# A 16-stage network on one core: the steps of its first attention in a written order, with the projections copied out of PSUM

## Chip, cores, metric

One NeuronCore of a Trainium2 chip. The metric is the device time of one execution in microseconds (us). All tensors of this stage are float32.

## The reference, cut to what matters

The network takes a tensor of 8 sequences ("batches", b) x 512 tokens x 128 features through sixteen layers, attention and feed-forward in turn, each behind a layer norm and with a residual. The change touches the first layer, a causal linear attention with 16 heads of 8 features:

```python
x = L0_attn_a_X                                    # (8, 512, 128)
x = x + _L0_attn_a_ref(_layernorm(x), Wq, Wv, q_norm_w, v_norm_w)
x = x + _L0_ffn_ref(_layernorm(x), ...)            # mixture of experts, top 2 of 8

def _L0_attn_a_ref(X, Wq, Wv, q_norm_w, v_norm_w):
    K = X.reshape(B, L, H, d)
    Q = rms_norm_multihead((X @ Wq.T).reshape(B, L, H, d), q_norm_w)
    V = rms_norm_multihead((X @ Wv.T).reshape(B, L, H, d), v_norm_w)
    W = jnp.cumsum(jnp.einsum('blhd,blhe->blhde', K, V), axis=1)
    return jnp.einsum('blhd,blhde->blhe', Q, W).reshape(B, L, D)
```

The keys are the normalised input itself. Queries and values are projected and RMS-normalised per head. Nothing of the mathematics changes.

## The kernel before

**Tiling.** A batch of 512 tokens is four tiles of 128 tokens; a tile t is 128 partitions x 128 features. For each batch the stage does two groups of steps and a tail.

*Begin steps* (`begin_steps`, L306 on): layer norm of the batch (`self.norm`, L202: statistics on VectorE L198 and L199, the root on GpSimd L180 and L184, the scaling on VectorE L207); transposes of the four tiles into one PSUM bank (L255) and a copy out by ScalarE (L257); `project(0)` and `project(1)`, each two tiles times the query and value weights (L316), squared by ScalarE (L326) and summed per head by VectorE (L327); `scales` (VectorE L337, the root on ScalarE L339, VectorE L341 to L344); `normalise(0)` and `normalise(1)`, which multiply the projections, read from PSUM, by the scales into `q` (L352) and into a block-diagonal value tile `vm` (L359, two buffers, one for even and one for odd batches); `queries` (transposes L369, four ScalarE copies with a head mask into `qm`, L375, and one into `qT`, L376).

*Chunk steps* (`chunk_steps`, L389 on), per tile t: `scores(t)` (TensorE L397 into two double-bank PSUM tiles `sc`, of which the pool holds two; half of them is masked and copied out by VectorE L406, the other half is copied by ScalarE L409 and masked by GpSimd L410); `carry(t)` (TensorE L423, VectorE L431, for t > 0 GpSimd L433), the running state; `weigh(t)` (for t > 0 TensorE L442, then 32-column matmuls L453) into one PSUM bank `o` that stays open for all four tiles; `copy` (ScalarE L464).

*Tail*: `finish` (transposes L470 and VectorE L174, the residual), then the steps in `ended`, which are the layer norm and the router scores of the mixture of experts that follows: statistics (L198, L180, L184), the shift (VectorE L239), the scaling (ScalarE L244), a store of the normalised batch to DRAM (issued by ScalarE's queue, L553), the transposes (L255, L257), and the router's matmuls (L561) with their sum on VectorE (L571).

**What sets the order.** The stage is under a manual schedule: every engine runs its instructions in the order in which the Python code issues them and waits at the head of its queue until the inputs and the buffer of the next one are there. The Python order is made by `together` (L498): the chunk steps of batch b are spread evenly, the tail of batch b-1 over the first 80% of them, the begin steps of batch b+1 over all of them. The main round of batch b thus holds the chunk steps of b, the tail of b-1 and all begin steps of b+1; these must be done before the next round begins with `scores(0)` of b+1. A step with several engines issues to all of them at once. The pool of single PSUM banks holds four; each half of a projection holds one from `project` until `normalise` has read it, and `o` holds one through the round.

After the last batch's tail the mixture of experts begins with VectorE work on the router scores of all batches (L620 on).

Of the kernel before, what the change touches and what calls it, by code (L numbers as in the profile page):

```python
# [22 lines left out]
F32 = mybir.dt.float32  # L23
# [6 lines left out]
P = 128  # L30
B, S, D, H, HD = 8, 512, 128, 16, 8
NT = S // P
# [4 lines left out]
LN_EPS = 1e-5  # L37
# [45 lines left out]
class Net:  # L83
# [102 lines left out]
    def stats(self, src, eps):  # L186

        nc = self.nc
        mv = self.moments(src)
        rs = self.small([P, NT], "rstd")  # L190
        self.rsqrt(rs, mv[:, :, 1], eps)
        return mv, rs
# [83 lines left out]
        return o.rearrange("p (t d) -> p t d", t=NT)  # L276


    def linear_attention(self):

        nc = self.nc
        w = self.weights("l0a_w")
        with self.tc.tile_pool(name="l0a", bufs=2) as pool, self.tc.tile_pool(
            name="l0a_fix", bufs=1
# [20 lines left out]
            def begin_steps(b, box):  # L307
                xT = self.xTb(b)
                vm = vms[b % 2]

                def project(half):
                    ps = self.av()
                    box["ps", half] = ps
                    for k in range(2):
                        t = 2 * half + k
                        nc.tensor.matmul(  # L316
                            ps[:, k * 256 : (k + 1) * 256],
                            lhsT=xT[:, t * P : (t + 1) * P],
                            rhs=w[:, 0:256],
                            start=True,  # L320
                            stop=True,
                        )
                    if half == 0:
                        box["ss"] = pool.tile([P, P], F32, tag="ss", name="ss")
                    sq = pool.tile([P, 512], F32, tag="sq", name="sq")
                    nc.scalar.activation(sq, ps, AF.Square)  # L326
                    nc.vector.tensor_reduce(  # L327
                        box["ss"][:, half * 64 : (half + 1) * 64],
                        sq.rearrange("p (n d) -> p n d", d=HD),
                        AX.X,  # L330
                        ALU.add,
                    )

                def scales():

                    ss = box["ss"]
                    nc.vector.tensor_scalar(ss, ss, 1.0 / HD, 1e-8, ALU.mult, ALU.add)  # L337
                    r = pool.tile([P, P], F32, tag="r", name="r")
                    nc.scalar.activation(r, ss, AF.Sqrt)  # L339
                    r0 = pool.tile([P, P], F32, tag="r0", name="r0")  # L340
                    nc.vector.reciprocal(r0, r)  # L341
                    nc.vector.tensor_tensor(r, r0, r0, ALU.mult)
                    nc.vector.scalar_tensor_tensor(r, r, -0.5, ss, ALU.mult, ALU.mult)
                    nc.vector.scalar_tensor_tensor(r, r, 1.5, r0, ALU.add, ALU.mult)  # L344
                    box["r"] = r.rearrange("p (t n) -> p t n", t=NT)

                def normalise(half):
                    ps = box["ps", half].rearrange("p (t n d) -> p t n d", t=2, d=HD)
                    r = box["r"][:, 2 * half : 2 * half + 2, :]
                    if half == 0:  # L350
                        box["q"] = pool.tile([P, NT, P], F32, tag="q", name="q")
                    nc.vector.tensor_tensor(  # L352
                        box["q"][:, 2 * half : 2 * half + 2, :].rearrange("p t (n d) -> p t n d", d=HD),
                        ps[:, :, 0:H, :],
                        bc(r[:, :, 0:H], 3, HD),
                        ALU.mult,
                    )
                    for k in range(2):
                        nc.vector.tensor_tensor(  # L359
                            diagonal(vm, 2 * half + k),  # L360
                            ps[:, k, H:32, :].rearrange("p (j r) d -> p r j d", j=4),
                            bc(r[:, k, H:32].rearrange("p (j r) -> p r j", j=4), 3, HD),
                            ALU.mult,
                        )

                def queries():
                    pt = self.m()
                    for t in range(NT):
                        nc.tensor.transpose(pt[:, t * P : (t + 1) * P], box["q"][:, t, :], self.ident)  # L369
                    qm = pool.tile([P, NT, 4, P], F32, tag="qm", name="qm")  # L370
                    box["qm"] = qm
                    box["qT"] = pool.tile([P, S], F32, tag="qT", name="qT")
                    v = pt.rearrange("p (t q) -> p t q", t=NT)
                    for r in range(4):
                        nc.scalar.activation(qm[:, :, r, :], v, AF.Copy, scale=pick[:, r : r + 1])  # L375
                    nc.scalar.activation(box["qT"], pt, AF.Copy, scale=cols[:, 0:1])  # L376

                return [
                    lambda: self.norm(self.xnb(b), self.xb(b)),
                    lambda: self.transposed(xT, self.xnb(b), act=True),  # L380
                    lambda: project(0),
                    lambda: project(1),
                    scales,
                    lambda: normalise(0),
                    lambda: normalise(1),
                    queries,
                ]

            def chunk_steps(b, box):  # L389
                xT, xn, vm = self.xTb(b), self.xnb(b), vms[b % 2]  # L390

                def scores(t):
                    tok = slice(t * P, (t + 1) * P)
                    ss = [self.sc() for _ in range(2)]
                    for j in range(4):
                        rows = slice(32 * j, 32 * j + 32)
                        nc.tensor.matmul(  # L397
                            ss[j // 2][:, j % 2, :],
                            lhsT=xT[rows, tok],
                            rhs=box["qm"][rows, t].rearrange("p r q -> p (r q)"),  # L400
                            start=True,
                            stop=True,
                        )
                    es = [pool.tile([P, 8, P], F32, tag=f"e{k}", name=f"e{k}") for k in range(2)]
                    box["e", t] = es
                    nc.vector.tensor_tensor(  # L406
                        es[0], ss[0].rearrange("p j (r q) -> p (j r) q", r=4), bc(self.cc(C_LIN, P), 1, 8), ALU.mult
                    )
                    nc.scalar.copy(es[1], ss[1].rearrange("p j (r q) -> p (j r) q", r=4))  # L409
                    nc.gpsimd.affine_select(  # L410
                        out=es[1],
                        in_=es[1],
                        pattern=[[0, 8], [1, P]],
                        compare_op=ALU.is_ge,
                        fill=0.0,
                        base=0,
                        channel_multiplier=-1,
                    )
# [51 lines left out]
                        nc.tensor.transpose(pt[:, tok], box["oT"][:, tok], self.ident)  # L470
                    self.add_x(b, pt.rearrange("p (t d) -> p t d", t=NT))

                steps = [lambda: scores(0), lambda: carry(0)]
                for t in range(1, NT):
                    steps += [lambda t=t: scores(t), lambda t=t: weigh(t - 1)]
                    if t < NT - 1:
                        steps.append(lambda t=t: carry(t))
                return steps + [lambda: weigh(NT - 1), copy], finish

            box = {}  # L480
            for f in begin_steps(0, box):
                f()
            tail = None
            for b in range(B):
                main, finish = chunk_steps(b, box)
                sides = []
                if b:
                    sides.append((0.8, [tail] + self.ended(b - 1)))
                if b + 1 < B:
                    box = {}  # L490
                    sides.append((1.0, begin_steps(b + 1, box)))
                self.together(main, *sides)
                tail = finish
            for f in [tail] + self.ended(B - 1):
                f()

    @staticmethod
    def together(main, *sides):  # L498


        at = [((i + 1) / len(main), 0, f) for i, f in enumerate(main)]
        for k, (to, side, *rest) in enumerate(sides):
            begin = rest[0] if rest else 0
            at += [((i + 0.5) / len(side) * (to - begin) + begin, k + 1, f) for i, f in enumerate(side)]
        for _, _, f in sorted(at, key=lambda x: x[:2]):
            f()

# [2100 lines left out]
```

## Time and profile before

| | us |
|---|---|
| median of 3 runs (3680.75 to 3695.16) | 3685.98 |
| the profiled execution | 3678.17 |
| its span, first to last instruction | 3676.3 |
| first projection matmul (L316) starts | 24.29 |
| last router matmul (L561) of the stage ends | 251.97 |
| from one `qm` copy (L375) to the next, batches 3 to 7 | 27.4 |

Times inside the run are counted from the start of the span. The stage is the stretch from 24 to 252 us, 6% of the span. A table by windows gives for each stretch the busy time of each engine (number of instructions in brackets) and the share of full speed that TensorE's clock was granted ("PEclk"). The chain of waits is followed back from the last instruction: at each step to what released it, or to the instruction before it on its engine. Its lines are start, length and what ran; "x8" is eight instructions in a row. TensorE runs each float32 matmul as two instructions, so the four matmuls of `scores(t)` are "x8".

### The profile page before, as it was taken

What the parts mean: (1) busy time and instruction counts of PE and PEld (TensorE: products, weight loads), DVE (VectorE), ACT (ScalarE), POOL (GpSimd) and SP (SyncE); (2) the same over time, 40 slices, a digit from 0 to 9 for tenths busy, and PEclk for the clock granted to TensorE, in tenths of its full rate; (3) what the DMA queues carried; (4) which work ended last, traced back from release to release, by engine and by line L of the source; (5) the groups of instructions that cost most, each with busy time, mean ns of one, the idle gap of its engine ahead of it and who ended that gap; (6) DMA issues with size and microseconds to landing.
All of it is one profiled execution on the core that took longest, in us unless ns stands there. A gap on an engine that the chain in (4) does not pass through costs nothing.

```text
span 3676.3 us, 64102 instructions
## 1 busy us (share of the span) xinstructions
PE 2920.8 (79%) x21332; PEld 1897.3 (52%) x21332; DVE 2503.5 (68%) x7103; ACT 2061.9 (56%) x4054; POOL 1857.4 (51%) x2494
## 2 busy tenths in 40 slices
PE   5757928999958747585655799999999999998886
PEld 3436912333327736483555455666556566555554
DVE  4555328888744357633443689999888899877984
ACT  3422325777732333153333477788887777776773
POOL 3313443332114466244134477667777877665775
PEclk8877958999978967787878899999999999997997
DMA  2001232222001301020013212111121111200000
GB/s 90 13 14 39 66 95 69 65 63 67 28 14 52 102 28 29 15 55 26 27 39 97 83 70 72 67 69 64 62 73 63 57 68 59 74 15 1 7 7 12
DMA packets 129802, 185.03 MB, mean 50 GB/s; under 512 B 19010, under 2 KB 98498, under 8 KB 129478
## 3 DMA queue, kind: packets, MB, share of 16 engines
q1 hardware_dynamic: 98886, 134.27, 10.8%
q0 software_dynamic: 15616, 35.47, 3.7%
q10 hardware_dynamic: 14976, 11.19, 1.1%
q8 instruction: 176, 2.88, 0.3%
q14 instruction: 148, 1.21, 0.1%
HBM read 128.40 MB, written 52.46 MB: 49 GB/s over the span
## 4 chain that ended last, share of the span: by engine, by line
PE 37%; DVE 19%; POOL 15%; DMA 13%; ACT 8%; issue 4%; SPq 2%; another core or an unknown queue 0%; DVEq 0%; ACTq 0%; POOLq 0%
DMA k<-d 9%; PE sc L744 5%; PE av L760 5%; PE av L1065 4%; PE mx L953 3%; PE sc L1034 3%; POOL e L1047 2%; DVE nm L972 2%; ACT e L1044 2%; PE m L255 2%; DMA d<-thirds 2%; SPq L926 2%; POOL left L911 1%; PE up L1321 1%; POOL got L811 1%
## 5 line engine op out<-in xcount | busy, mean ns | idle before, releaser
L1044 ACT ACTIVATE e<-sc 128x1024 f32<-128x1024 f32 (+1 forms) x832 | 745.1, 930 | 158.5 <-PE sc L1034 119.4
L965 DVE TENSOR_REDUCE pm<-mx 128x4 f32<-128x512 f32 (+1 forms) x1152 | 626.2, 592 | 86.5 <-PE mx L953 84.5
L953 PE MATMUL mx<-k,q 126*128 126x512 bf16 (+3 forms) x2048 | 551.3, 327 | 117.0 <-DMA k<-d 104.4
L1034 PE MATMUL sc<-q,k 128*128 128x512 bf16 (+3 forms) x2048 | 446.3, 322 | 20.4 <-ACT e L1044 18.8
L1047 POOL TENSOR_SCALAR_AFFINE_SELECT e<-e 128x256 f32<-128x256 f32 x768 | 295.2, 406 | 198.5 <-ACT e L1044 195.7
L723 POOL DMA_INDIRECT xg<-xd,srci x220 | 210.3, 956 | 365.6 <-DVE srci L716 192.1
L972 DVE TENSOR_REDUCE nm<-mx 128x1 f32<-128x512 f32 x512 | 324.3, 683 | 83.9 <-PE mx L953 81.4
L1065 PE MATMUL av<-e,vaug 128*32 128x512 f32 (+3 forms) x4096 | 366.9, 479 | 1.9 <-ACT e L1044 1.8
L953 PEld LDWEIGHTS <-q 126*128 126x128 bf16 x2048 | 198.0, 99 | 327.1 <-issue 254.3
L255 PE MATMUL m<-ident,xn 128*128 128x128 f32 x480 | 109.7, 339 | 245.8 <-ACT xn L223 117.1
L950 PE MATMUL mx<-maskbf,identbf 128*128 128x128 bf16 (+1 forms) x1152 | 268.4, 238 | 16.6 <-DVE h L1346 6.6
L1034 PEld LDWEIGHTS <-k 128*128 128x128 bf16 x2048 | 181.5, 99 | 190.3 <-issue 116.7
L760 PE MATMUL av<-moe_w,h 128*128 x1760 | 239.7, 281 | 10.6 <-issue 6.2
L744 PE MATMUL sc<-xgT,w1c 128*128 128x128 f32 x1760 | 243.3, 283 | 3.9 <-DVE w1c L732 3.5
L244 ACT ACTIVATE xn<-x,ln_shift,rstd 128x128 f32<-128x128 f32 x416 | 171.9, 495 | 111.3 <-DVE ln_shift L239 97.2
L811 POOL DMA_INDIRECT got<-yd,posi x192 | 191.2, 996 | 76.7 <-issue 68.7
L744 PEld LDWEIGHTS sc<-xgT,w1c 128*128 128x128 f32 x1760 | 225.4, 200 | 4.2 <-issue 3.7
L760 PEld LDWEIGHTS av<-moe_w,h 128*128 128x128 f32 x1760 | 220.3, 196 | 13.1 <-issue 8.1
L255 PEld LDWEIGHTS m<-ident,xn 128*128 128x128 f32 x480 | 69.2, 162 | 284.4 <-ACT xn L223 134.4
L1065 PEld LDWEIGHTS av<-e,vaug 128*32 128x32 f32 x4096 | 108.3, 109 | 184.8 <-issue 146.0
L732 DVE COPY w1c<-moe_w 128x516 f32 x220 | 101.0, 459 | 137.1 <-issue 80.5
L747 ACT ACTIVATE h<-sc 128x512 f32<-128x512 f32 x142 | 84.8, 597 | 169.5 <-PE sc L744 154.6
(429 smaller groups left out, 6566.1 us busy)
## 6 DMA issues: line engine op xcount, KB each, us to landing
q<-d SPq DMA_DIRECT2D x128, 288.0 KB
k<-d SPq DMA_DIRECT2D x384, 96.0 KB
d<-thirds SPq DMA_DIRECT2D x48, 384.0 KB
yd<-y SPq DMA_DIRECT2D x220, 64.0 KB
xd<-xn ACTq DMA_DIRECT2D x24, 256.0 KB
d<-thirds SPq DMA_DIRECT2D x48, 128.0 KB
moe_w<-in_moe_w POOLq DMA_DIRECT2D x8, 516.0 KB
moe_w<-in_moe_w POOLq DMA_DIRECT2D x8, 512.0 KB
```

The source lines that it names most:

```text
L255: nc.tensor.transpose(pt[:, t * P : (t + 1) * P], src[:, t, :], self.ident)
L744: nc.tensor.matmul(ps[:, cols], lhsT=w1c[i][:, cols], rhs=xgT[i], start=True, stop=True)
L760: nc.tensor.matmul(ps[:, 0:P], lhsT=h[i][:, c * P : (c + 1) * P], rhs=w2[:, bass.ds(e + c * P, P)], start=c == 0, stop=c == 3,)
L811: nc.gpsimd.indirect_dma_start(got[b][k][:, i, :], None, yd, bass.IndirectOffsetOnAxis(ap=posi[:, j : j + 1], axis=0))
L950: nc.tensor.matmul(out, lhsT=self.identbf, rhs=mask, start=True, stop=False, skip_group_check=True)
L953: nc.tensor.matmul(s[:, col : col + n], lhsT=q[:, t, :], rhs=key[:, 0 : n // P, :], start=not causal, stop=True, skip_group_check=True,)
L965: nc.vector.tensor_reduce(box["pm"][:, h, at : at + n // P], s[:, 0:n].rearrange("p (k n) -> p k n", n=P), AX.X, ALU.max,)
L972: nc.vector.tensor_reduce(box["nm"][:, u, h : h + 1], s, AX.X, ALU.max, negate=True)
L1034: nc.tensor.matmul(s[:, jj, col : col + n], lhsT=key[:, t, :], rhs=q[:, at // P : (at + n) // P, :], start=True, stop=True,)
L1044: nc.scalar.activation(e, s[:, :, 0:wide], AF.Exp, scale=scale)
L1047: nc.gpsimd.affine_select(out=e[:, :, col : col + P], in_=e[:, :, col : col + P], pattern=[[0, 2], [1, P]], compare_op=ALU.is_ge, fill=0.0 ...
L1065: nc.tensor.matmul(acc[g][32 * j : 32 * j + 32, at : at + n], lhsT=vaug[:, t, first : first + 32], rhs=pair[j // 2][:, j % 2, col : col + ...
```

## The change

1. A string `LINEAR` gives the order of the steps for one round; the number behind a name is the lag, so `s1:2` in round i is `scores(1)` of batch i-2. `in_order` (already used by other stages, L1730) goes through rounds 0 to 10. A batch is normed in round b, projected and given its first scores and state in round b+1 (`t`, `p0` to `q`, `s0`, `c0`), weighed in round b+2, and ended in round b+3. `together` is deleted.
2. The steps are cut finer: `norm` into `n0` (statistics) and `n1` (scaling); `scales` into `r0` (up to the root) and `r1`; the tail uses `ended(b, True)`: `e0` statistics, `e1` shift, `e2` scaling, `e3` transposes, `e4` router matmuls, `e5` their sum, `e6` the store, which is now issued by SyncE's queue instead of ScalarE's.
3. After the squares, ScalarE copies each projection (128 x 512) from PSUM into an SBUF tile `raw0` or `raw1` (one buffer each), and `normalise` reads that in place of PSUM.

```python
def in_order(self, order, parts, n=B, late=None):
    order = [(n, int(k or 0)) for n, _, k in (w.partition(":") for w in order.split())]
    ...
    for i in range(n + gap + max(k for _, k in order)):
        for name, k in order:
            b = i - k
            ...
            if 0 <= b < n:
                ...
                if name in made[b]:
                    made[b][name]()
```

```diff
+    LINEAR = """
+        t:1 s1:2 w0:2 f:3 c1:2 p0:1 p1:1 e0:3 s2:2 r0:1 w1:2 c2:2 r1:1 e1:3 s3:2 v0:1 e2:3 w2:2 v1:1 e6:3
+        q:1 n0 w3:2 o:2 n1 e3:3 e4:3 s0:1 c0:1 e5:3
+    """
...
                 def project(half):
-                    ps = self.av()
-                    box["ps", half] = ps
+                    ps = self.m()
...
+                    raw = box["raw", half] = pool.tile([P, 512], F32, tag=f"raw{half}", name=f"raw{half}", bufs=1)
                     sq = pool.tile([P, 512], F32, tag="sq", name="sq")
                     nc.scalar.activation(sq, ps, AF.Square)
+                    nc.scalar.copy(raw, ps)
...
-                def scales():
-
+                def roots():
                     ss = box["ss"]
                     nc.vector.tensor_scalar(ss, ss, 1.0 / HD, 1e-8, ALU.mult, ALU.add)
-                    r = pool.tile([P, P], F32, tag="r", name="r")
+                    r = box["r"] = pool.tile([P, P], F32, tag="r", name="r")
                     nc.scalar.activation(r, ss, AF.Sqrt)
+
+                def scales():
+                    ss, r = box["ss"], box["r"]
...
                 def normalise(half):
-                    ps = box["ps", half].rearrange("p (t n d) -> p t n d", t=2, d=HD)
+                    raw = box.pop(("raw", half)).rearrange("p (t n d) -> p t n d", t=2, d=HD)
...
-                        ps[:, :, 0:H, :],
+                        raw[:, :, 0:H, :],
...
-                            ps[:, k, H:32, :].rearrange("p (j r) d -> p r j d", j=4),
+                            raw[:, k, H:32, :].rearrange("p (j r) d -> p r j d", j=4),
...
-            for b in range(B):
-                main, finish = chunk_steps(b, box)
...
-                self.together(main, *sides)
...
+            def parts(b):
+                box = {}
+                out = {**begin_steps(b, box), **chunk_steps(b, box)}
+                out.update({f"e{k}": f for k, f in enumerate(self.ended(b, True))})
+                return out
+
+            self.in_order(self.LINEAR, parts)
```

More of the change, by code (lines that the diff above doesn't have):

```diff
@@ L376, in queries, with stats @@
                     nc.scalar.activation(box["qT"], pt, AF.Copy, scale=cols[:, 0:1])
[L378 to L387, printed above, removed]
+                def stats():
+                    box["at"] = self.stats(self.xb(b), LN_EPS)
+                return {
+                    "n0": stats,
+                    "n1": lambda: self.scaled(self.xnb(b), self.xb(b), *box.pop("at")),
+                    "t": lambda: self.transposed(xT, self.xnb(b), act=True),
+                    "p0": lambda: project(0),
+                    "p1": lambda: project(1),
+                    "r0": roots,
+                    "r1": scales,
+                    "v0": lambda: normalise(0),
+                    "v1": lambda: normalise(1),
+                    "q": queries,
+                }
             def chunk_steps(b, box):
@@ L471, in finish @@
                     self.add_x(b, pt.rearrange("p (t d) -> p t d", t=NT))
-                steps = [lambda: scores(0), lambda: carry(0)]
-                for t in range(1, NT):
-                    steps += [lambda t=t: scores(t), lambda t=t: weigh(t - 1)]
+                steps = {"o": copy, "f": finish}
+                for t in range(NT):
+                    steps[f"s{t}"] = lambda t=t: scores(t)
+                    steps[f"w{t}"] = lambda t=t: weigh(t)
                     if t < NT - 1:
[L477 to L483, printed above, removed]
-            for b in range(B):
-                main, finish = chunk_steps(b, box)
[L486 to L491, printed above, removed]
-                self.together(main, *sides)
[L493 to L506, printed above, removed]
+                        steps[f"c{t}"] = lambda t=t: carry(t)
+                return steps
+            def parts(b):
[4 more added lines that the diff above has]
+            self.in_order(self.LINEAR, parts)
     W1 = HID + 4
```

## The prediction

> **What bounds the kernel now.** I read the busy time by windows first: the stage as a whole, and one main round of it.
>
> ```profile
> 24.00:252.00 228.00, 164.77 (x1628) 101.01 (x1628) 122.28 (x332) 95.93 (x153) 61.67 (x80) 0.81 0.05 13
> 138.96:166.36 27.40, 20.35 (x204) 12.72 (x204) 15.41 (x43) 11.68 (x19) 7.70 (x11) 0.81 0.04 11
> ```
>
> The columns are length, then busy PE, PEld, DVE, ACT, POOL, then the granted clock. In a round of 27.40 us no engine is full: TensorE is busy 20.35, VectorE 15.41. So waits set the round, and I read the chain for the same round.
>
> ```profile
> 138.96 2.42 ACT qm L375 x4
> 141.39 0.58 ACT qT L376
> 141.97 0.59 ACT oT L464
> 142.60 0.66 PE m L470 x4
> ...
> 152.64 0.60 ACT sq L326
> 153.26 0.69 DVE ss L327
> 153.95 1.13 DVE e L406
> 155.75 0.96 DVE r L341
> 157.94 1.88 PE m L561 x8
> 159.82 2.02 PE sc L397 x8
> ...
> 166.36 2.42 ACT qm L375 x4
> ```
>
> TensorE stands still twice: 3.6 us while ScalarE makes qm, qT and oT, and some 3 us while VectorE reduces the squares and makes the scales. And two lines are slow: the router matmuls take 1.88 us here, 0.85 at 236.28, and `scores` takes 2.02, 1.07 elsewhere. The clock is why:
>
> ```profile
> 99.20:102.61 3.41, 0.59 (x6) 1.00 0.00 0
> 102.61:106.02 3.41, 2.99 (x16) 0.50 0.01 2
> 106.02:109.44 3.42, 3.42 (x42) 0.50 0.00 0
> 109.44:112.85 3.41, 2.09 (x42) 1.00 0.02 5
> 112.85:116.26 3.41, 1.05 (x8) 1.00 0.00 0
> 116.26:119.68 3.42, 3.42 (x18) 0.50 0.00 0
> 119.68:123.09 3.41, 3.41 (x48) 1.00 0.00 0
> ```
>
> (length, PE busy, clock.) The clock changes only on a fixed grid of 3.41 us. After a window with little PE work (0.59 or 1.05 of 3.41) the next runs at half speed; 2.09 keeps full speed; it comes back only after a window that is all but full (2.99 was not enough). Each round pays three half-speed windows. At the full-speed durations of the chain's rows a round holds 15.8 us of PE work, so half speed costs it some 4.6 us.
>
> **The change, part by part.** *Copies out of PSUM* add 16 ScalarE copies of 128x512 PSUM to SBUF. The row of the same shape is L257's, 594 ns: 9.5 us of ScalarE in all, 1.2 a round, which ScalarE (11.68 of 27.40 busy) has room for. One thing lies on a path: in the first round, with nothing else running, `raw1` sits between the squares and the root, +0.55 us. If ScalarE had no room, the cost would be those 9.5 us. In exchange the two banks are free after about 1.2 us; o and three rotating banks are then enough, and I find no bank that is waited for. `normalise` now reads two SBUF operands. L359 takes 279 ns from PSUM and L342, two SBUF operands and the same 128x128, 292: +0.05 us a round.
>
> *The store* moves from ScalarE's queue (0.37 to 0.38 us of issue, 8 times, squares waiting behind it) to SyncE's. SyncE issues nothing else between 25.4 us and the stage's end, so nothing queues behind it; ScalarE gains 0.4 us a round.
>
> *The order.* I walked one full new round engine by engine, in the order of the string, each instruction starting when its engine and its inputs are free, lengths from the rows (start to next start where they follow back to back), at full clock. Time 0 is the end of the previous round's `c0`. The walk closes in a loop through four pieces:
>
> 1. PE. `s1` waits until 0.83 for VectorE to have read `s0`'s scores (L406, 1.22); then s1 1.07, w0 1.00, f 0.60, c1 0.42, p0 and p1 0.88 each: 5.7.
> 2. Square (L326) 0.61 and reduce (L327) 0.69: 7.1. VectorE is in line from here on: `e0` 1.72 (four pairs, L198 and L199), s2's L406 1.14, L337 0.41: 10.4. Root on ScalarE 0.34; `r1` 1.85; `e1` 0.20; s3's L406 1.14; v0 0.73; the first part of v1 0.41: 15.1.
> 3. `q` on PE 0.65, then ScalarE: qm and qT 3.0, oT 0.6, and xT for `e3` 0.6: 20.0.
> 4. PE `e4` 0.85, s0 1.07, c0 0.42: 22.4.
>
> So T = 22.4 us at full clock against 27.40. Off this loop lie w1, c2, w2, w3, e3, e2 and `n0`/`n1`. TensorE still waits three times: about 8.8 to 10.2 (s3 waits for L406 to empty a score tile), 12.8 to 15.2 (q), 17.9 to 20.0 (e4 waits for xT, and s0 and c0 wait behind it). ScalarE waits at the root, and s2's copy is past by then; the GpSimd mask of s2 waits behind e0's root until 11.3, which w2 meets.
>
> Now the clock. Between 8.8 and 20.0 PE has 5.2 us of work, so one window below half is certain; the grid decides which. If the window ends in 14.7 to 16.9 (about two thirds of the positions), half speed lasts over e4, s0, c0 and the beginning of t and s1: +1.03, +0.95, +0.30, +0.4: T = 25.1. If it ends in 19.7 to 21.5, one window of half speed follows: +1.6, T = 24.0. Mean 24.8. Bounds for T: 22.4, and 27.4 if nothing is gained.
>
> *Fill and drain.* The first scores and state of batch 0 end at 39.4 now, 40.0 with raw1. Round 2 has no tail: without e0 and e4 the walk gives 17.4, with half speed 20. Six full rounds, 3 to 8. Round 9 (last weighing, tail of batch 6) 14.3, with half speed 16. The last tail is as now, 242.4 to 252.0: 9.6. Sum: 40 + 20 + 6T + 16 + 9.6 = 85.6 + 6 x 24.8 = 234.4 against 252.0: **17.6 us less**. The router scores start the next layer's VectorE work, so all of it comes through. The profiled execution took 3678.17 with a span of 3676.3, so 3660.6 on its scale; it lies 7.8 below the median, and 3685.98 - 17.6 gives **3668**.
>
> **The rivals.**
>
> *The clock holds* (chance 0.12). Two rows speak for it: TensorE's share of work rises to 15.8 of 22.4 us, and 2.09 of 3.41 kept the clock. Against it: 1.05 of 3.41 did not, and the gap at 12.8 to 15.2 leaves a window with 0.96. Sum 40 + 17.4 + 6 x 22.4 + 14.3 + 9.6 = 215.7: 36 less, 3650. The Trainium skill, "TensorE: Matmul & The Clock Gate", section "What's actually happening", has the clock fall after an idle window of some 3.4 us; none of my three gaps is that long, so by its words this is the case that comes. The trace does not agree: the window with 1.05 us of work was not idle, and half speed followed.
>
> *VectorE is held up by GpSimd where it now reads two SBUF operands* (0.10).
>
> ```profile
> L1448 DVE SCALAR_TENSOR_TENSOR xr<-xn,rms_rs,l3b_rows x32: 319/381/1144, 3295.5 to 3546.3; 128x128 f32<-128x128 f32 x32
> L843 DVE TENSOR_TENSOR x<-x,got x8: 691/692/1640, 1296.6 to 1471.8; 128x512 f32<-128x512 f32 x8
> ```
>
> (shortest, median, longest ns.) Such instructions sometimes take 0.8 to 0.95 us longer. v0 and v1 are in the loop: up to 1.1 us, one GpSimd mask (L410), for each, T = 27.0, the sum 247.6, 4.4 less, 3682. Against it: in my walk GpSimd is idle from 13.6, when s3's mask ends, to 17.2, and v0 and v1 run from 14.0 to 15.5. The Trainium skill, "SBUF — State Buffer", section "SBUF: two separate sides", says why it could: a VectorE instruction with two SBUF inputs and a GpSimd one that reads SBUF lock each other out for a whole instruction. The two rows above fit that without proving it.
>
> *No shorter round* (0.08): hand-offs that I priced at 0.02 to 0.07 us, some 25 in the loop, cost 0.2 each, T = 27.4, 2 less: 3684.
>
> *Slower: half speed for good* (0.10). TensorE works in shorter pieces than now, and if a wait of 0.4 us falls into every 3.4 us, no window is full and the clock never returns. Then the loop's PE pieces are at half speed: 9.2 in place of 4.9 in piece 1, +0.45 for q, 4.63 for 2.34 in piece 4: T = 29.5. The sum is 40 + 24 + 6 x 29.5 + 20 + 11 = 272, 20 more: 3706. It is slower from T = 27.7 on. Against it: e4 to p1 is one stretch of 8 us at full clock, 14.7 at half, with one wait of 0.3 that vanishes at half speed, and every such stretch in the old round brought the clock back.
>
> **How the numbers follow.** The forecast has 0.60, with its own range 3658 to 3680 (T from 23.2 to 26.8). About 0.5%, 18.4 us, is what can be told from no change; the forecast's 17.6 lies on that edge, so half of it counts as faster. Faster: 0.30 + 0.12 = 0.42. Same: 0.30 + 0.10 + 0.08 = 0.48. Slower: 0.10. The range reaches to "the clock holds" and "no shorter round", with 2 and 6 us for the spread of runs (3680.75 to 3695.16): 3648 to 3690.
>
> **What would show it.** In the changed profile the four qm copies (L375's successor) should come 24 to 25.2 us apart in rounds 3 to 8, the last router matmul end near 234, TensorE wait for q and for the router's xT by 2 us or more, with one or two half-speed windows a round in place of three. ScalarE's busy time should rise by 9.5 us, PSUM banks release nobody late. A VectorE row of `q<-raw` well above 414 ns means the second rival; scores at 2.0 us throughout, the last. A round of 22.5 or less means that the clock held or that the walk has a wait too many; more than 27 that it lacks one.

## The result, and the profile after

The changed kernel takes 3671.37 us (median of 6 runs, 3666.24 to 3679.67), the kernel before 3691.85 (median of 6, 3680.75 to 3695.73): ratio 0.995, 95% interval 0.993 to 0.997, or 20.5 us less. Predicted were 3668 us and 17.6 us less. The profiled execution of after took 3679.67 us (span 3678.0). It is the slowest of its six, and the profiled one of before, 3678.17, is below all six of its own, so those two totals show no gain. The stage shows it.

First the busy time by windows of after, the stage and one main round (length, then busy PE, PEld, DVE, ACT, POOL, then granted clock):

```profile
24.00:234.00 210.00, 159.47 (x1628) 99.25 (x1628) 127.49 (x335) 103.20 (x169) 61.93 (x80) 0.84 0.05 14
126.35:150.45 24.10, 18.85 (x206) 11.86 (x205) 16.07 (x45) 12.63 (x21) 7.82 (x10) 0.85 0.04 11
```

The last router matmul (now L558) ends at 233.17 us, 251.97 before, 234.4 predicted. The round is 24.10 where it was 27.40. ScalarE is busy 103.20 in the stage against 95.93: the 16 copies cost 7.3, or 0.46 each, because each follows a square without a gap (starts 139.37 and 139.83). The chain of waits of after, for the same round:

```profile
126.35 2.42 ACT qm L386 x4
...
129.93 0.48 ACT xT L257
...
130.46 1.06 PE m L558 x8
131.51 1.79 PE sc L413 x8
133.30 0.73 PE m L439 x2
134.03 0.85 PE m L255 x4
134.88 1.21 PE sc L413 x8
...
139.83 0.62 ACT sq L333
...
144.38 0.96 DVE r L352
145.37 0.49 DVE r L353
...
146.50 0.96 DVE ln_shift L239
...
149.73 0.70 PE m L380 x2
```

These are the steps of the walk in its order: q copies and xT on ScalarE, router and `s0` on TensorE, `s1`, the projections, the second square, VectorE's line down to `v1`, the q transposes (L380), and the next `qm` at 150.45. Two lines are foreign to the walk: `sc` takes 1.79 in place of 1.07 (clock), and `ln_shift`, the step `e1`, takes 0.96 in place of 0.20. A third is a little longer, the first product of `r1` (L353): 0.49 for 0.29. The time that TensorE waits between 60 and 215 us (total, times, longest):

```profile
PE m L380 <- DVE q L363: 15.8, 9, 2.5
PE sc L413 <- DVE e L422: 9.3, 8, 1.4
PE m L558 <- ACT xT L257: 7.1, 6, 1.4
```

The three predicted waits and no others: q, a score tile, the router's xT. No single PSUM bank is among them. Last, the grid of the clock (length, PE busy, clock):

```profile
121.49:124.90 3.41, 0.92 (x33) 1.00 0.00 0
124.90:128.32 3.42, 3.37 (x38) 0.50 0.26 77
128.32:131.73 3.41, 2.07 (x24) 1.00 0.00 0
131.73:135.14 3.41, 3.41 (x18) 0.50 0.00 0
135.14:138.56 3.42, 3.42 (x50) 1.00 0.02 5
138.56:141.97 3.41, 3.41 (x48) 1.00 0.00 0
141.97:145.38 3.41, 2.04 (x20) 1.00 0.00 0
145.38:148.80 3.42, 1.12 (x33) 1.00 0.00 0
148.80:152.21 3.41, 3.17 (x34) 0.50 0.28 82
```

Two half-speed windows a round in place of three. The one that begins at 124.90 lies mostly under the q copies, when ScalarE sets the loop: TensorE is busy in it (3.37 of 3.42), but apart from the q transposes (0.70 for 0.45 at full clock) that work is off the loop. The one at 131.73 lies over `s0`, `c0` and the transposes.

Why did the profiled total not fall? The 18.8 us gained at the stage's end are lost later, some 10 of them in the last attention, where the code is the same. After:

```profile
3358.00:3584.00 226.00, 196.53 (x970) 128.07 (x969) 187.65 (x561) 159.92 (x446) 146.30 (x170) 0.83 0.02 6
```

and before:

```profile
3366.00:3582.00 216.00, 182.68 (x968) 119.17 (x968) 186.95 (x560) 159.95 (x446) 146.18 (x169) 0.90 0.02 6
```

The same work takes 226 or 216 us, at a clock of 0.83 or 0.90. Of two executions of the kernel before on one chip (3665.39 and 3651.24) the distance is 14 us. So a single total says little here, and I judge experiments by the end of the last router matmul of the stage ("the stage's end"), which three executions of after put at 233.17, 231.88 and 233.36.

### The profile page after: what moved, and what is told of

Read it like the earlier page. It is cut to its first block, busy times and chain, and to the rows that moved or that the text cites. A ratio compares the mean times of both kernels' runs of the same rounds, so it can differ in the third digit from the quotient of the medians.

```text
span 3678.0 us, 64011 instructions
## 1 busy us (share of the span) xinstructions
PE 2931.8 (80%) x21216; PEld 1910.3 (52%) x21332; DVE 2503.7 (68%) x7103; ACT 2067.3 (56%) x4070; POOL 1859.9 (51%) x2494
## 3 DMA queue, kind: packets, MB, share of 16 engines
q14 instruction: 148, 1.21, 0.1%
## 4 chain that ended last, share of the span: by engine, by line
PE 38%; DVE 20%; POOL 13%; DMA 12%; ACT 9%; issue 5%; SPq 2%; another core or an unknown queue 0%; DVEq 0%; ACTq 0%; POOLq 0%
DMA k<-d 8%; PE av L757 5%; PE sc L741 5%; PE av L1062 5%; PE mx L950 3%; PE sc L1031 3%; ACT e L1041 2%; DVE nm L969 2%; POOL e L1044 2%; PE m L255 2%; DMA d<-thirds 2%; SPq L923 1%; DVE bnst L198 1%; POOL got L808 1%; POOL left L908 1%
## 5 line engine op out<-in xcount | busy, mean ns | idle before, releaser
L1031 PE MATMUL sc<-q,k 128*128 128x512 bf16 (+3 forms) x1932 | 425.2, 319 | 23.5 <-ACT e L1041 19.0
L947 PE MATMUL mx<-maskbf,identbf 128*128 128x128 bf16 (+1 forms) x1152 | 268.3, 238 | 18.8 <-DVE h L1343 6.7
L180 POOL TENSOR_SCALAR rstd<-bnmv 128x4 f32<-128x4 f32 x152 | 35.9, 236 | 292.2 <-DVE bnmv L199 265.6
```

The lines of the kernel that those rows point to most:

```text
L947: nc.tensor.matmul(out, lhsT=self.identbf, rhs=mask, start=True, stop=False, skip_group_check=True)
L1031: nc.tensor.matmul(s[:, jj, col : col + n], lhsT=key[:, t, :], rhs=q[:, at // P : (at + n) // P, :], start=True, stop=True,)
```

## The experiments

The runs were made in three groups, each on a chip of its own; totals are compared only within a group. "Main rounds" are the distances between `qm` copies once the rounds are full.

| kernel | stage ends, us | main rounds, us | clock in the stage | total, us |
|---|---|---|---|---|
| group 1: before (no profile) | | | | 3691.34 |
| order_alone | 228.86 | 22.7 to 25.4 | 0.86 | 3662.11 |
| copies_alone | 237.64 | 23.8 to 25.7 | 0.85 | 3670.44 |
| shift_late | 221.64 | 21.9 to 23.2 | 0.89 | 3655.41 |
| fill | 226.87 | 23.9 | 0.91 | 3663.52 |
| group 2: before (before_again) | 252.23 | 27.4 | 0.81 | 3665.39; 3651.24 |
| after_again | 231.88 | 24.1 to 26.0 | 0.82 | 3644.25 |
| shift_late_no_copies | 222.02 | 21.8 to 23.0 | 0.85 | 3630.67 |
| five_rounds | 197.04 | 18.6 | 0.93 | 3602.09 |
| group 3: before, median of 11 | | | | 3658.17 |
| after_timed, median of 6 | 233.36 | 24.1 to 26.0 | 0.84 | 3635.34 |
| five_rounds_timed, median of 5 | 195.39 | 18.6 | 0.96 | 3600.55 |
| store_act | 230.86 | 24.0 to 25.9 | 0.82 | 3640.09 |
| five_rounds_no_copies | 195.98 | 18.2 to 18.9 | 0.93 | 3601.24 |

**order_alone: the new order without the copies.** The normalisation reads PSUM again; order and store are those of after.

```diff
-                    raw = box["raw", half] = pool.tile([P, 512], F32, tag=f"raw{half}", name=f"raw{half}", bufs=1)
+                    box["raw", half] = ps
                     nc.scalar.activation(sq, ps, AF.Square)
-                    nc.scalar.copy(raw, ps)
```

> The new order with the projections left in PSUM until they are scaled, as before. Theory A (the order makes the whole gain; the open bank o, the two held banks and one more are just enough for c2, the only step between p1 and v1 that takes a bank): the last router matmul ends within 2 us of the changed kernel's 233.2, ScalarE busy some 9 us less, the first qm copies 0.5 us earlier, rounds of 24 to 26 us. Theory B (the copies are what lets the order work): TensorE waits for a bank between p1 and q, each round at least 1 us longer, the stage ends at 241 or later.

The stage ends at 228.86, 23.1 before the old order's and 4.3 before that of after. That is outside the 2 us of theory A and far from the 241 of theory B: the order makes the gain by itself. One of its rounds, from the chain:

```profile
124.38 2.42 ACT qm L385 x4
...
129.55 1.08 PE sc L412 x8
...
130.65 1.24 DVE e L421
...
131.93 1.14 PE sc L412 x8
...
136.72 0.61 ACT sq L333
...
143.37 0.96 DVE ln_shift L239
...
146.58 0.45 PE m L379 x2
...
147.06 2.42 ACT qm L385 x4
```

This round of 22.68 us has its only half-speed window at 124.3 to 127.7, under the q copies, so all that counts runs at full clock. Laid beside the round of 24.10 of after it says where the 1.42 between them lie: `s0` 1.08 for 1.79, the q transposes 0.45 for 0.70, the way from `s0` to `s1` 1.30 for 1.58, `s1` 1.14 for 1.21. These 1.31 are clock. The copy between the squares costs what is left, 0.1: TensorE's second projection ends at 139.64 in after and its square starts at 139.83; here the two stand at 136.62 and 136.72. So in this pair of rounds the difference is nearly all clock, which window fell to half speed, and hardly any of it the copies' own work. That most of the 4.3 us is the same is my reading of this one pair.

**copies_alone: the old order with the copies.** Projections go to the pool `m`, are copied to `raw0` and `raw1` behind the squares, and the normalisation reads those; `together` and the store are those of before.

```diff
-                    ps = self.av()
-                    box["ps", half] = ps
+                    ps = self.m()
...
                     nc.scalar.activation(sq, ps, AF.Square)
+                    raw = box["ps", half] = pool.tile([P, 512], F32, tag=f"raw{half}", name=f"raw{half}", bufs=1)
+                    nc.scalar.copy(raw, ps)
```

> The old order with the copies out of PSUM. Theory A (no bank was waited for in the old order; the copies only add 1.2 us a round to ScalarE, in front of the score copies and the second square): the last router matmul ends between 252 and 262, rounds of 27.4 to 28.6 us. Theory B (held banks were a hidden wait of the old order): it ends before 247, rounds under 27.

The stage ends at 237.64: the copies alone win 14.3 us in the old order, where my prediction gave them a cost and no gain in time. The PE waits of before (60 to 215 us) say why:

```profile
PE m L470 <- ACT oT L464: 18.4, 5, 3.7
PE m L561 <- DVE state L431: 16.6, 6, 2.8
PE m L423 <- ACT xT L257: 3.9, 6, 0.9
```

and the three largest of copies_alone:

```profile
PE m L471 <- ACT oT L465: 25.7, 7, 3.7
PE av L454 <- DVE e L407: 6.7, 5, 2.0
PE m L562 <- ACT xT L257: 5.1, 6, 1.0
```

In each round of before the router's matmul waits 2.8 us for `state` (L431), a product that it does not read. What it needs is the PSUM bank that this product reads. The product stands in VectorE's line behind the scales, and of the other three banks `o` holds one and the two projections hold two until they are normalised. The third line is of the same kind: `carry` (L423) reads `xn` and `vm`, and yet waits up to 0.9 us for ScalarE's copy of `xT`, which empties the bank used before it. With the copies out of PSUM both waits are gone. (That it is the bank is inferred from this; that the waits go with the copies is what the run shows. The clock rose too, from 0.81 to 0.85, and its part of the 14.3 us was not separated.) It was in the profile that I had, and I read it as the time for the scales. The same run shows a price, in the timeline:

```profile
127.69 1.64 DVE L360 TENSOR_TENSOR vm<-raw,r 128x128 f32<-128x128 f32 x2
128.04 1.15 POOL L411 TENSOR_SCALAR_AFFINE_SELECT e<-e 128x1024 f32<-128x1024 f32 x1
```

Two products that took 0.48 us where nothing stood beside them take 1.64, and the second ends 0.14 behind GpSimd's mask. This is the predicted second rival, in the old order.

**shift_late: `e1` behind `s3`.** One step is moved; nothing else differs from after.

```diff
-        t:1 s1:2 w0:2 f:3 c1:2 p0:1 p1:1 e0:3 s2:2 r0:1 w1:2 c2:2 r1:1 e1:3 s3:2 v0:1 e2:3 w2:2 v1:1 e6:3
+        t:1 s1:2 w0:2 f:3 c1:2 p0:1 p1:1 e0:3 s2:2 r0:1 w1:2 c2:2 r1:1 s3:2 e1:3 v0:1 e2:3 w2:2 v1:1 e6:3
```

> The changed kernel with e1 (the shift, 4 numbers a partition) one place later in the order, behind s3. In the changed kernel its row is 1.04 us and ends with the GpSimd mask of s3 that runs beside it; in the kernel before it takes 0.2 to 0.35. Theory A (VectorE with two SBUF operands is held up until the GpSimd instruction ends): its row falls to 0.2, VectorE reaches s3's scores 0.8 us sooner, rounds 0.5 to 1.5 us shorter, the last router matmul at 224 to 230. Theory B (the shift is slow because its input from GpSimd is late, or its length has another cause): the row stays near 1 us and the stage ends within 2 us of 233.2.

The row of L239 in after (shortest, median, longest ns), and below it the timeline at one of the six:

```profile
L239 DVE SCALAR_TENSOR_TENSOR ln_shift<-bnmv,rstd x6: 1044/1046/1047, 72.9 to 196.6; 128x4 f32<-128x4 f32 x6
```

```profile
122.20 1.15 POOL L426 TENSOR_SCALAR_AFFINE_SELECT e<-e 128x1024 f32<-128x1024 f32 x1 [0.60 <-ACT e L425]
122.32 1.04 DVE L239 SCALAR_TENSOR_TENSOR ln_shift<-bnmv,rstd 128x4 f32<-128x4 f32 x1
```

The same row in shift_late, and below it in before:

```profile
L239 DVE SCALAR_TENSOR_TENSOR ln_shift<-bnmv,rstd x7: 151/152/154, 73.0 to 207.6; 128x4 f32<-128x4 f32 x7
L239 DVE SCALAR_TENSOR_TENSOR ln_shift<-bnmv,rstd x6: 197/388/737, 66.3 to 205.0; 128x4 f32<-128x4 f32 x6
```

An instruction with four elements a partition takes 1.04 us, and always 1.04, because it starts 0.12 behind the GpSimd mask of `s3` and ends with it. Behind VectorE's own copy of `s3` it takes 0.15. The row of before shows that the hold-up is not new: there `e1` takes anything from 0.20 to 0.74 us (not 0.2 to 0.35, as I wrote above), depending on where it meets a GpSimd mask, and each of the six ends within 0.02 us of that mask's end (at 66.35 it takes 0.74, to 67.09; the mask runs from 65.98 to 67.07). The rounds of 24.1 become mostly 23.0 to 23.2 and the stage ends at 221.64, 11.5 earlier: some 0.9 a round is the hold-up, in seven rounds 6, and the rest is clock (0.89 for 0.84), which was not separated further.

**fill: matmuls that nobody reads.** Before q and before `e4` TensorE gets 12 and 6 bf16 matmuls of 128x256 that only keep it busy.

```diff
+                def fill(n):
+                    ps = self.m()
+                    for _ in range(n):
+                        nc.tensor.matmul(ps[:, 0:256], lhsT=self.identbf, rhs=self.maskbf, start=True, stop=True)
...
-        ... e2:3 w2:2 v1:1 e6:3 q:1 n0 w3:2 o:2 n1 e3:3 e4:3 s0:1 c0:1 e5:3
+        ... e2:3 w2:2 z0:1 v1:1 e6:3 q:1 n0 w3:2 o:2 n1 e3:3 z1:1 e4:3 s0:1 c0:1 e5:3
```

> The changed kernel with idle matmuls (128x256 bf16, into a PSUM bank that nobody reads): 12 between w2 and q, 6 between e3 and e4, where TensorE waits 2.5 and 1.4 us. Theory A (half speed costs 1.2 to 3 us a round because those waits leave a clock window under half full): the granted clock of the stage rises from 0.84 to 0.93 or more, scores takes 1.07 us wherever it stands, rounds fall to 22 to 23.3 us, the last router matmul ends at 219 to 227. Theory B (the clock is not what lengthens the loop, or the idle matmuls stand in the way): the stage ends at 232 or later.

The clock of the stage rises from 0.84 to 0.91, a little short of the 0.93 expected (the round from 122.56 to 146.47 us has 0.93), and the stage ends at 226.87, 6.3 earlier; the rounds stay at 23.9, seven windows of the grid, not the 22 to 23.3 expected, for one half-speed window a round is left and one `scores` still takes 2.09. That idle time of TensorE costs clock is borne out; what the last window costs stays open.

**shift_late_no_copies: both edits together.**

> The changed kernel without the copies out of PSUM and with e1 behind s3. Theory A (the two costs are separate: the copies put raw0 in front of the second square, the early shift waits for GpSimd): 3 to 5 us less than with e1 behind s3 alone, the last router matmul at 216 to 219.5. Theory B (they hide each other, or held banks begin to stall once the round is shorter): 221 or later.

222.02, no better than shift_late alone, at a clock of 0.85 for 0.89: theory A missed, and the end is where theory B put it, but no single PSUM bank is among TensorE's waits. What the copies cost in order_alone's pair does not add up with the rest.

**after_again and before_again.**

> The changed kernel once more. Its profiled execution ended the stage 18.8 us earlier than the kernel before, yet its span was 1.7 us longer; 9 us of that were lost in the last attention (3366 to 3582), at a granted clock of 0.83 against 0.90. Theory A (chance of the clock grid, new in each execution): the stage again ends within 2.5 us of 233.2, and the total differs from the first by 4 us or more. Theory B (the change itself slows later stages): the stage ends at 233 and the total is again 3677 to 3682.

> The kernel before once more. Theory A (later stages scatter by the clock grid): the last router matmul of the stage ends within 2 us of 252.0, and the total lies in the band of its other runs, 3685 to 3696, above the 3678 of its first profiled execution. Theory B: the total is 3678 again.

The stage's ends come back within 1.3 and 0.3 us, on another chip, 20.4 apart. The totals of these two are 21.1 apart, but the other execution of before on this chip, 3651.24, lies only 7.0 above after_again: single totals settle little here too. The expected total of before, 3685 to 3696, did not hold there: this chip is faster on the whole kernel.

**store_act: the store of the normalised rows on ScalarE's queue again.**

```diff
-                return [stats, shift, apply, turn, score, keep, lambda: store(nc.sync)]
+                return [stats, shift, apply, turn, score, keep, lambda: store(nc.scalar)]
```

> The changed kernel with the store of the normalised rows back on ScalarE's queue, the third part of the change undone alone. Theory A (ScalarE waits over a us ahead of the q copies in each round, so its queue has room for one more issue): last router matmul within 2 us of the 231 to 233 of the changed kernel. Theory B (the issue lies ahead of a ScalarE step that TensorE waits for): 0.4 us more in each of 8 rounds, 234.5 to 237.

230.86, just before the 231.88 to 233.36 of after. Moving the store gained nothing here: ScalarE waits 1.3 us ahead of the q copies in any case.

**five_rounds: the tail one round later.** What the above suggests: `e1` out of VectorE's line between the second square and q, the router's transposes a round behind the scaling, `s0` right behind the last weighing.

```diff
-        t:1 s1:2 w0:2 f:3 c1:2 p0:1 p1:1 e0:3 s2:2 r0:1 w1:2 c2:2 r1:1 e1:3 s3:2 v0:1 e2:3 w2:2 v1:1 e6:3
-        q:1 n0 w3:2 o:2 n1 e3:3 e4:3 s0:1 c0:1 e5:3
+        t:1 e1:4 s1:2 e2:4 w0:2 f:3 c1:2 e0:3 p0:1 p1:1 s2:2 e6:4 e3:4 r0:1 w1:2 c2:2 r1:1 s3:2 e4:4 v0:1
+        w2:2 v1:1 e5:4 q:1 n0 w3:2 o:2 n1 s0:1 c0:1
```

> The changed kernel with another order: e0 (statistics of the tail) moves from behind p1 to behind c1, where VectorE waits for the squares, and e1 to e5 lag one round more, e1 and e2 to the beginning of the round, e3 behind s2, e4 behind s3; a batch then takes five rounds. Theory A (the loop of a round is what VectorE does in line between p1 and q, plus ScalarE's qm to xT and the router's matmuls behind them): e0, xT and e4 leave the loop, 1.7 + 0.6 + 0.9 to 1.1 us, TensorE's waits fall under 1.5 us and the clock holds, rounds of 18 to 20.5 us, the last router matmul ends at 186 to 203. Theory B (the round is bound by engine work or by hand-offs outside this loop): rounds of 22 us or more, the end at 215 or later.

> The five-round order again, now timed. Theory A (what the one look showed is the kernel, not the chip): last router matmul at 196 to 198 us, and the whole faster than the kernel before by the 55 us that the stage's end comes earlier, less up to 14 us of scatter of the later stages: ratio 0.984 to 0.989. Theory B (the later stages give the gain back, as a part of it was in the changed kernel's profiled run): the stage ends at 197 but the ratio is above 0.991.

> The changed kernel unaltered, timed on the same chip as the five-round order. Theory A (the gain of the change is the stage's 18 to 21 us): ratio 0.993 to 0.996 to the kernel before, and the five-round order 30 to 38 us below it. Theory B (the later stages move with the order too): outside 0.992 to 0.997.

Timed: 3600.55 us, ratio 0.9838 (0.982 to 0.9857) to the kernel before, with after at 0.9939 (0.9921 to 0.9958) on the same chip. The stage ends at 195.39, 38.0 before after's, and the medians are 34.8 apart; so most of the stage's gain reaches the end. Both are a little better than the 196 to 198 and 0.984 to 0.989 of theory A. One round of the timed run, then the stage:

```profile
114.66:133.24 18.58, 15.57 (x211) 10.08 (x204) 15.59 (x44) 12.45 (x22) 7.84 (x10) 1.00 0.05 16
24.00:196.00 172.00, 135.54 (x1628) 85.49 (x1628) 125.93 (x334) 102.25 (x169) 62.06 (x80) 0.96 0.06 17
```

and its chain through that round:

```profile
113.46 1.05 POOL rstd L184
...
114.54 1.11 DVE xn L207 x4
115.66 1.15 DVE e L422
...
122.11 1.16 DVE ss L335 x2
123.27 1.13 DVE e L422
124.40 0.62 DVE ss L345
...
128.45 0.33 DVE q L363
```

The round runs wholly at full clock, TensorE is busy 15.57 of 18.58, and but for the root on ScalarE the chain is VectorE's own line from 119.6 to 131.6: another bound than before. Less VectorE work should move it; no run here tried that. `e1` still meets a GpSimd mask in some rounds (L239 takes 0.17 to 1.06 us), but in the round shown VectorE waits 0.58 us for TensorE soon after it, so it costs nothing there.

**five_rounds_no_copies.**

> The five-round order with the normalise reading PSUM and no copies. Theory A (VectorE's own line sets these rounds, and it reads PSUM as fast as the copies): rounds of 18.3 to 18.9 us, last router matmul within 3 us of 197. Theory B (held banks make TensorE wait again, as they did in the order before the change): rounds above 19.5 us, end above 204. Theory C (ScalarE's copies still lie on the path): rounds below 18.1 us, end below 193.

195.98, with rounds of 18.2 to 18.9, 18.5 on average. In this order the copies are worth nothing either way.

## Why the prediction was right, and where it was wrong

**The walk and the clock: right.** Piece by piece it gave 22.4 us for a round at full clock, and the round of order_alone in which full clock held where it counts is 22.68. VectorE's line from the second square to q is 9.86 there where I had 9.4; q is shorter, 0.45 for 0.65. With half speed I had 24.0 to 25.1, mean 24.8. The `qm` copies of rounds 3 to 8 follow the ones before by 21.13, 25.56, 24.10, 24.10, 24.16 and 25.99 us: mean 24.2, with two half-speed windows in the round shown, where one or two were named. The 21.13 is outside the 24 to 25.2 that I gave as a sign: the first tail's router steps come behind the `q` of round 3, so they fall into the next distance. Two lie above it. Fill and drain: the first `qm` comes at 34.6 instead of 34.1, 34.2 without copies, so the +0.55 is 0.3 to 0.5. Round 2 ends with `c0` at 60.5 (60 predicted), the six full rounds take 147.0 from there, 24.5 each (24.8 predicted), and from the end of the last `c0` (207.5) to the stage's end are 25.7 us (25.6 predicted). So each term of the sum holds, and not only the total.

**The router's wait for xT: too long.** I put 2.1 us there, and at least 2 as the sign; it is at most 1.4. The loop is the same whichever engine is ahead, so T did not suffer.

**The second rival: the mechanism right, the place wrong.** I looked for VectorE held up by GpSimd at the two normalisations, because those read SBUF for the first time, found GpSimd idle there in the walk, and gave it 0.10. Their rows keep to 407 to 424 ns in after. But the step `e1`, which I priced at 0.20, the shortest of a row of before that goes up to 0.74, also reads two SBUF operands, and the walk itself has it at 12.6 to 12.8, ahead of the 13.6 at which `s3`'s mask ends. I did not look there. In the run `e1` waits that mask out in every full round, 0.85 us each, and it stands in the loop. The first product of `r1` (L353) is held up too: 0.48 us in each full round, beside GpSimd's addition to the state (L449, 0.46 us), where it took 0.29 in before. Together that is some 1.0 us a round that I had not priced. It was covered by pieces that I had too long (`e0` took 1.60 for 1.72, the step before the root 0.14 for 0.41), and by the range; that they nearly cancel is luck.

**The copies: the term in the new order right, what they are for missed.** I had no path cost but the first round's. In the new order that holds within what the runs can tell: 0.1 us a round directly, 4.3 in one pair, mostly clock by the rounds compared, nothing in two other pairs. A copy cost 0.46 us, not 0.594, so ScalarE's busy time rose by 7.3 and not 9.5. But "I find no bank that is waited for" was said only of the new order; in the old one a bank was waited for 2.8 us a round, behind a releaser that makes no sense as data. Order and copies each take that wait away, 23 and 14 us alone, and together 19 to 20, not 37.

**The store: no effect, as far as can be seen.** I had ScalarE gain 0.4 us a round; store_act shows no gain. And SyncE does issue one other transfer before the stage's end, 0.36 us at 206.02 in before, which I had left out; nothing in the runs shows that it mattered.

**The clock does not hold, nor does it stay at half: right to give both little.** "The clock holds" (T 22.4, 215.7 at the stage's end) asked that short gaps keep full speed; 0.92 and 1.12 us of work in a window did not. "Half speed for good" asked for waits in every window; the half-speed window at 131.73 is full of work (3.41), and behind it the clock is back.

**Stage to total: right.** The stage gave 18.8 in the profiled pair and 20.4 in a second, the medians 20.5 and 22.8.

## What to carry to other kernels

When an instruction waits for one whose result it does not read, ask which buffer the other one is reading: a PSUM bank that another engine has yet to read looks like data in a list of waits. Two edits that take the same wait away are not to be added up. And when steps are put in a written order, look at what GpSimd does beside each VectorE step with two SBUF operands, however small the step is, and read the longest of its row as well as the shortest.

## What the runs showed of the hardware

**A small VectorE instruction can wait a whole GpSimd one out.** 128x4 elements took 0.15 us alone and 1.04 beside a mask of 1.15; 128x128 took 0.28 or 1.17, and 0.29 or 0.48 beside an addition of 0.46. The Trainium skill, "SBUF — State Buffer", section "SBUF: two separate sides", says that a VectorE instruction with two SBUF inputs and a GpSimd one that reads SBUF take an exclusive lock for their whole length, whoever starts first. These rows agree as far as they go: the VectorE instruction that starts second ends with the GpSimd one or up to 0.14 us behind it. The other way round was not looked at.

**The clock falls without an idle window.** A window with 0.92 us of TensorE work was followed by half speed, and one with 1.12. The Trainium skill, "TensorE: Matmul & The Clock Gate", section "What's actually happening", asks for an idle window of some 3.4 us; this trace differs, and the trace decides. Busy time by itself doesn't settle the middle: 2.07 lost the clock at 131.73, while full speed went on behind the 2.04 of the window at 141.97 to 145.38. Why is open.

**Rounds stick near the grid.** Rounds of 23.9 (fill) and 24.0 to 24.1 (most of after and store_act) are close to seven windows of 3.413 us, 23.9; a round that is freed of half speed by its place on the grid took 22.7, and the next one 25.4. If the grid holds them there, a saving of 0.1 or 0.4 us a round can come out as nothing or as several times its size. That it does is my reading; no run here moved the grid alone, and the rounds of shift_late (21.9 to 23.2) and of the five-round order (18.6) lie at no whole number of windows.
